# Four recurrent layers on one core: layer 0's first chain moved from GpSimd to VectorE, and layer 2's inside-chunk weights held without the quarter that causality makes zero

## The chip, the cores and the metric

One core of one Trainium2 chip. The metric is the device time of one execution in microseconds (us), on the one core that the kernel uses. Three executions of the kernel before took 1184.43, 1192.12 and 1193.15 us (median 1192.12). A change of 1% is about 12 us.

## The reference, cut to what matters

The program is four layers over X of shape 2 batches x 1024 positions x 128 features; each layer computes `x = x + s * silu(g)` with a sequence part `s` and a mixture or feed-forward part `g`. Two places matter here.

Layer 0 normalises x, adds a gated residual, quantises it in groups, normalises again (`u`) and runs a selective scan (Mamba) on it. Its step size passes through a softplus before the scan can begin:

```
xs = silu(conv(u @ in_proj.T))            # 4 taps
dt, B, C = split(xs @ x_proj.T)
dt = softplus(dt @ dt_proj.T + dt_b)
h = h * exp(dt * A) + dt * x * B          # per position: the scan
```

Layer 2 is a state-space layer with 32 heads of 64 values and a state of 128. The kernel cuts the 1024 positions into 8 chunks of 128. Inside a chunk the output is a product with a weight matrix per head, zero where the source comes after the target:

```
M[s, l] = (B_s . C_l) * exp(sum of A*dt over s < k <= l)    for s <= l, else 0
Y_diag[l] = sum over s of M[s, l] * dt_s * h_s
Y_off[l]  = (C_l . state before the chunk) * exp(sum of A*dt up to l)
y = (Y_diag + Y_off + D*h) * silu(gate), then a norm and W_out
```

M has 128 sources (s) by 128 targets (l) per chunk. For targets in the first half of a chunk, the sources of the second half are all zero: that is one quarter of M.

## The kernel before, in words

The kernel is written layer by layer, but the order in which each engine works is not the order of the text. `_operations` (line 153) collects every instruction with a cost (`_price`, line 104), `_forward` (line 259) plays the program out with these costs, the tiles' buffers and the semaphores' lags, `_backward` gives each operation how much work still hangs on it, and `_issue_order` (line 433) runs both in turn 30 times, then 300 times with random changes of the keys, and keeps the shortest order that its own costs give. That order is forced on all engines. So a change in one place can reorder the whole program. Costs for PE in `_price`: a plain f32 product takes 8 ns plus 4 x 0.4167 ns for each column of the moving operand; of products that write 64, 32 or 8 partitions, those that follow each other into the same tile (`mate`, line 213) are counted as running beside each other, and the last of them takes 87 ns more. A change between array shapes elsewhere has no cost in the plan.

Layer 0 begins with four stages per 512 positions (normalise, turn, gate, residual), then `quantise`, then the parts of the scan's input for one half of a batch (512 positions): `take_1` (line 1000: statistics, inverse root, `u`, its transpose and the split in two f32r halves `uT_h`, `uT_l`), `take_2` (taps and silu), `take_3` (projection, `dt`), `take_4` (line 1071: softplus, `dt` to DRAM) and `take_5`. `statistics` (569) calls `inverse_root` (579): three Newton steps, which for four columns (`small_pool`) run on GpSimd as 12 small instructions (lines 595 to 598), and else on VectorE as 9 (591 to 593). In `take_1` the four `u` (line 1007) are GpSimd's, in `take_4` two operations for each half of the channels (1080, 1081). The scan (`step`, 1246) cannot begin before `take_4` of the first half is through and `dd` has come back by DMA. Beside all this run the steps of layer 0's mixture of experts (`first`, `second`, `third`, `weighted_sum`, lines 1127 to 1162).

Layer 2 works in 32 blocks (2 batches x 16 blocks; a block is 128 feature rows, two heads). `batch_start` (1487) makes, once per batch, B and C, the products `GT` of B and C in each chunk (1510, 1512), and the sums of A*dt as rows that it writes to DRAM (`Vd`, `Cd`, `So`). For each block, `front` (1659) makes h and the gate, `weights` (1684) M, `states` (1704) the chunk states, and `tail` (1740) the output. In the main loop `front` and `weights` run two blocks ahead of `tail`.

`weights`: two small DMAs bring the rows of the two heads (`Srow` from `Cd`, `Mrow` from `Vd`); for each half of the chunks two products over 512 columns (line 1698) make the exponents of both heads in PSUM, ScalarE takes exp over 1024 columns (1699), VectorE multiplies with `GT` (1701) into `M`, 128 partitions x 1024. `tail`: for each half (`q`) of the positions, eight products with 64 output partitions each (line 1757, two heads side by side, 128 sources, 128 targets) into `yd`, four with all 128 partitions (1762) into `yo`; VectorE adds D*h (1765) and multiplies by the decay (1767); GpSimd adds and gates (1768, 1769); ScalarE squares. `yd`, `yo` and `wo` share two PSUM banks (tag `y_ps`). Every fourth block the gated blocks go through `W_out` (1781).

All DMAs are issued by SP, one queue in order.

Of the kernel before, what the change touches and what calls it, by code (L numbers as in the profile page):

```python
# [10 lines left out]
F32 = mybir.dt.float32  # L11
# [8 lines left out]
P = 128  # L20
# [131 lines left out]

def _operations(nc, slots):
# [6 lines left out]
    for ins in nc.cur_bb.bb.instructions:  # L160
# [7 lines left out]
        if ins.opcode == "Matmult" and not ins.is_transpose and writes[0].ap[0][1] in (8, 32, 64):  # L168
            op.strip, op.area = writes[0].offset // (writes[0].ap[0][0] or 1), 1.0
            op.columns, op.strips = {(op.strip, writes[0].offset)}, {op.strip}  # L170
# [43 lines left out]
        if op.columns and mate is not None and mate.columns and mate.tiles[-1] == op.tiles[-1] and not mate.columns & op.columns:  # L214
            op.columns |= mate.columns
            if op.strip in mate.strips:
                op.cost += 10.0
            else:
                op.strips |= mate.strips
                op.cost = 25.0  # L220
            first = mate.first
            first.after.update({o: max(lag, first.after.get(o, -1e3)) for o, lag in op.after.items() if o.at < first.at})
            mate.mate, op.first = op, first
# [235 lines left out]
def recurrent_d4(ctx: ExitStack, tc: tile.TileContext, x, w0, f0, fwd, w1, w13d, w1y, w2, w2in, w3, r0, r2, r3, out):  # L459
# [109 lines left out]
    def statistics(src, ts):  # L569

        n = len(ts)
        st = small.tile([P, n, 6], F32, name=f"ln_st{n}")
        mv = small.tile([P, n, 2], F32, name=f"ln_mv{n}")
        for i, t in enumerate(ts):
            nc.vector.bn_stats(st[:, i, :], src[:, t, :])
            nc.vector.bn_aggr(mv[:, i, :], st[:, i, :])
        return mv, inverse_root(mv[:, :, 1], f"ln{n}")

    def inverse_root(v, name):

        n = v.shape[-1]
        small_pool = n == 4
# [7 lines left out]
        for _ in range(0 if small_pool else 3):  # L590
            nc.vector.tensor_tensor(t, y, y, ALU.mult)  # L591
            nc.vector.scalar_tensor_tensor(t, t, -0.5, x, ALU.mult, ALU.mult)
            nc.vector.scalar_tensor_tensor(y, t, 1.5, y, ALU.add, ALU.mult)
        for _ in range(3 if small_pool else 0):
            nc.gpsimd.tensor_tensor(t, y, y, ALU.mult)
            nc.gpsimd.tensor_tensor(t, t, x, ALU.mult)
            nc.gpsimd.tensor_scalar(t, t, -0.5, 1.5, ALU.mult, ALU.add)
            nc.gpsimd.tensor_tensor(y, t, y, ALU.mult)
# [226 lines left out]
    with ExitStack() as l1, ExitStack() as l0:  # L825
# [52 lines left out]
        with pool_of("l0a") as pa, pool_of("l0b", bufs=2) as pb, pool_of("l0_pre", bufs=5, space=PSUM) as pp:  # L878
# [121 lines left out]
            def take_1(b, h, pp, tag):  # L1000

                ts = range(b * TPB + 4 * h, b * TPB + 4 * h + 4)
                mv, rinv = statistics(qx, ts)
                shift = shifted(mv, rinv)
                u = pj.tile([P, 4, D], F32, name="u")
                for j, t in enumerate(ts):
                    nc.gpsimd.tensor_scalar(u[:, j, :], qx[:, t, :], rinv[:, j : j + 1], shift[:, j : j + 1], ALU.mult, ALU.add)
# [63 lines left out]
            def take_4(b, h, pp, tag, fast=False):  # L1071
# [3 lines left out]
                for c in range(2):  # L1075
# [4 lines left out]
                    nc.gpsimd.tensor_scalar(w[:, c, :], e, 1.0, -1.0, ALU.add, ALU.add)  # L1080
                    nc.gpsimd.tensor_tensor(w[:, c, :], e, w[:, c, :], ALU.subtract)
# [29 lines left out]
            take_1(0, 0, pp, "mm")  # L1111
# [230 lines left out]
    with ExitStack() as l2, ExitStack() as lead:  # L1342
# [79 lines left out]
        with pool_of("w2early", side="right") as pe, pool_of("l2f", side="right") as pf, pool_of("l2fw", bufs=2, side="right") as pw, lead:  # L1422
# [42 lines left out]
            le_from = pa.tile([P, 4, P], F32, name="le_from")  # L1465
# [5 lines left out]
            for b in range(4):  # L1471
                nc.gpsimd.tensor_copy(le_32[:, 32 * b : 32 * (b + 1)], le_from[:, b, 32 * b : 32 * (b + 1)])

# [7 lines left out]
            Mrow = [pfr.tile([P, 4, P], F32R, name=f"Mrow{i}", bufs=1) for i in range(NR)]  # L1481
# [5 lines left out]
            def batch_start(b, room, pw, pp):  # L1487
# [15 lines left out]
                GT = pa.tile([P, TPB, P], F32, name=f"GT{b}")  # L1503
                for q in range(2):
                    ps = pp.tile([P, W], F32, name="bt_ps", tag="pre")[:, :512]
                    pg = pp.tile([P, W], F32, name="g_ps", tag="pre")[:, :512]
                    for j in range(4):
                        c = slice((4 * q + j) * P, (4 * q + j + 1) * P)
                        nc.tensor.transpose(ps[:, j * P : (j + 1) * P], Bf[:, c], ident)
                        nc.tensor.matmul(pg[:, j * P : (j + 1) * P], Bf[:, c], Cf[:, c], start=True, stop=True)  # L1510
                    nc.scalar.copy(Btok[:, 4 * q : 4 * q + 4, :], ps.rearrange("p (j d) -> p j d", d=P))
                    nc.vector.tensor_tensor(GT[:, 4 * q : 4 * q + 4, :], pg.rearrange("p (j d) -> p j d", d=P), le.unsqueeze(1).to_broadcast([P, 4, P]), ALU.mult)
# [7 lines left out]
                for half in range(2):  # L1520
                    ps = pp.tile([P, W], F32, name="v_ps", tag="pre")[:, :512]
                    pk = pp.tile([P, W], F32, name="k_ps", tag="pre")[:, :512]
                    for o, x, m, first, last in ((ps, Adt, le_from.rearrange("p b l -> p (b l)"), True, True), (pk[:, :P], Adt, le_32, True, False), (pk[:, :P], nlog, ident, False, True)):
# [3 lines left out]
                    pv = ps.rearrange("p (b l) -> p b l", b=4)  # L1527
                    v.append(room("v2", [P, 2, 4, P], F32R))
                    split(pv, v[half][:, 0], v[half][:, 1])
                    nc.scalar.activation(so[:, half, :], pv[:, 0, :], AF.Exp)  # L1530
                    yield
                    mark(f"start_2_{b}")
                Vd = pd.tile([4, NH, 2, 8, P], F32, name="Vd")
                Cd = pd.tile([NH, 2, 4, 2, P], F32, name="Cd")
                So = pd.tile([NH, 2, 4, P], F32, name="So")
                for half in range(2):
                    nc.sync.dma_start(Vd[:, :, half].rearrange("c h o l -> (c h) o l"), v[half].rearrange("p o b l -> p (o b) l").bitcast(F32))
                    nc.sync.dma_start(Cd[:, half].rearrange("h c o k -> c h (o k)"), csum[:, half].rearrange("p o k -> p (o k)").bitcast(F32))
# [59 lines left out]
            patm = pf.tile([8, 512], F32, name="patm", tag="rows")  # L1598
# [6 lines left out]
            pm1 = patm.rearrange("r (c l) -> r c l", c=4)  # L1605
            nc.gpsimd.memset(pm1, -1.0)
            for sign, off in ((1, 0), (-1, 1)):
                nc.gpsimd.affine_select(out=pm1, in_=pm1, pattern=[[-2 * sign, 4], [0, P]], compare_op=ALU.is_ge, fill=0.0, base=off, channel_multiplier=sign)
            for Sr, Mr in zip(Srow, Mrow):
                nc.vector.tensor_tensor(Sr[:32].rearrange("r g k -> r (g k)"), pat, pat2, ALU.add)  # L1610
                nc.vector.tensor_copy(Mr[32:40].rearrange("r c l -> r (c l)"), patm)
# [42 lines left out]
        with pool_of("l2mid") as pmid, pool_of("l2w", bufs=2) as pw, pool_of("l2end", bufs=3) as pend, pool_of("l2_in", bufs=2, space=PSUM) as pin, pool_of("l2_ps", bufs=2, space=PSUM) as pp:  # L1654
# [29 lines left out]
            def weights(b, i):  # L1684
# [7 lines left out]
                nc.sync.dma_start(Sr[32:40].bitcast(F32), Cd[hs].rearrange("h a c o k -> (c o) (h a) k"))  # L1692
                nc.sync.dma_start(Mr[:32].bitcast(F32), Vd[:, hs].rearrange("c h a o l -> (h a o) c l"))
                Ms = [pw.tile([P, 2, 512], F32, name="M", bufs=6) for _ in range(2)]
                for half, M in enumerate(Ms):
                    ps = pin.tile([P, 2, 512], F32, name="e_ps", tag="pre")
                    for h in range(2):
                        nc.tensor.matmul(ps[:, h, :], Sr[:, 2 * h + half, :], Mr.rearrange("r c l -> r (c l)"), start=True, stop=True)  # L1698
                    nc.scalar.activation(ps, ps, AF.Exp)  # L1699
                    G = GT[:, 4 * half : 4 * half + 4, :].rearrange("p j l -> p (j l)").unsqueeze(1).to_broadcast([P, 2, 512])  # L1700
# [3 lines left out]
            def states(b, i):  # L1704
# [4 lines left out]
                htok = pw.tile([P, TPB, P], F32, name="htok")  # L1709
                hdd = pmid.tile([P, TPB, P], F32, name="hdd")  # L1710
                cd = pmid.tile([P, 2, 2, HP * 4], F32, name="cd", bufs=2)
                nc.sync.dma_start(cd.rearrange("p a h w -> p a (h w)"), Dd[:, 2 * i : 2 * i + 2].rearrange("a h p j -> a (h p j)").partition_broadcast(P))
                for half in range(2):
# [8 lines left out]
                    nc.scalar.copy(htok[:, js, :], ps.rearrange("p (j f) -> p j f", j=4))  # L1722
                    nc.gpsimd.tensor_tensor(v(hdd[:, js, :]), v(htok[:, js, :]), by(dtd), ALU.mult)  # L1723
# [14 lines left out]
                mid_of[b, i] = (mid_of[b, i], htok, stc)  # L1738

            def tail(b, i):  # L1740
# [7 lines left out]
                Ms, htok, stc = mid_of.pop((b, i))  # L1748
                so = pend.tile([P, S], F32, name="so2")
                for k in range(2):  # L1750
                    nc.sync.dma_start(so[64 * k : 64 * (k + 1)], So[2 * i + k].rearrange("a c l -> (a c l)").partition_broadcast(64))
                for q in range(2):
                    cols = slice(512 * q, 512 * (q + 1))
                    yd = pp.tile([P, 512], F32, name="yd_ps", tag="y_ps")
                    for j in range(4):
                        for k in range(2):
                            nc.tensor.matmul(yd[64 * k : 64 * (k + 1), j * P : (j + 1) * P], htok[:, 4 * q + j, 64 * k : 64 * (k + 1)], Ms[q][:, k, j * P : (j + 1) * P], start=True, stop=True)  # L1757
                    yo = pp.tile([P, 512], F32, name="yo_ps", tag="y_ps")
                    for j in range(4):
                        c = 4 * q + j  # L1760
                        if c:
                            nc.tensor.matmul(yo[:, j * P : (j + 1) * P], stc[:, c - 1, :], Cf[:, c * P : (c + 1) * P], start=True, stop=True)  # L1762

                    y = h[:, cols]
                    nc.vector.scalar_tensor_tensor(y, y, W2["D"][:, i : i + 1], yd, ALU.mult, ALU.add)  # L1765
                    a = P if q == 0 else 0
                    nc.vector.tensor_tensor(so[:, 512 * q + a : 512 * (q + 1)], yo[:, a:], so[:, 512 * q + a : 512 * (q + 1)], ALU.mult)  # L1767
                    nc.gpsimd.tensor_tensor(y[:, a:], y[:, a:], so[:, 512 * q + a : 512 * (q + 1)], ALU.add)  # L1768
# [3 lines left out]
                    else:  # L1772
                        nc.scalar.activation(so[:, cols], y, AF.Square)  # L1773
                        nc.gpsimd.tensor_tensor(ssq[:, cols], ssq[:, cols], so[:, cols], ALU.add)  # L1774
# [41 lines left out]
            places = dict(Bf=("M", 6), v2=("M", 6), rows=("so2", 3), cdx=("cd", 2))  # L1816
# [231 lines left out]
```

## Time and profile before

| what | us |
|---|---|
| median of three executions | 1192.12 |
| the profiled execution: its own time | 1188.86 |
| its span, first to last instruction | 1187.1 |
| layer 0 (to about 460), of it before the first exp of the scan (line 1251) | 118.1 |
| layers 1 and the start of 2 | about 460 to 670 |
| layer 2's blocks | about 670 to 1095 |
| layer 3, whose first work lies beside the last blocks | to 1187 |

The page gives, per engine, the busy time and its share of the span, and by 40 slices how busy each engine was and the granted clock of TensorE (1.0 is full speed). PE is TensorE's matrix work, PEld its weight loads, which may run beside it; DVE is VectorE, ACT ScalarE, POOL GpSimd, SP the engine that issues DMAs. A f32 product appears as two records (x16 is eight products), an f32r product as one. The records' durations contain the way through the array, so how densely products follow each other is read from their starts. Over the whole span PE is busy 1020.7 us (86%), DVE 931.5 (78%), ACT 866.1 (73%), POOL 739.2 (62%). The granted clock is below full speed in some stretches between 100 and 450 us and between 600 and 692 us; from 700 us on it is 1.0.

### The profile page before, as it was taken

The page shows a single profiled execution, that of the slowest core. Times are in us where ns is not written, and L with a number is a line of the kernel's source. Part 1 is how long each engine was busy: PE and PEld are TensorE (multiplying, and loading weights), DVE is VectorE, ACT ScalarE, POOL GpSimd, SP SyncE. Part 2 cuts the span into 40 slices and gives each one's busy share as a digit, 9 for nine tenths or more (in the row PEclk, how much of TensorE's full clock was granted, in tenths as well). Part 3 has the DMA queues.
Part 4 walks back from the last instruction along what each step waited for, and adds up shares of the span by engine and source line. Part 5 has one row for each costly group of instructions (what it writes and reads, how often), then busy time and mean ns, then how long its engine had stood idle before and what let it go on. Part 6 is the DMA issues. An engine that isn't in the chain of part 4 may idle for free.

```text
span 1187.1 us, 18167 instructions
## 1 busy us (share of the span) xinstructions
PE 1020.7 (86%) x6399; PEld 735.6 (62%) x6399; DVE 931.5 (78%) x1537; ACT 866.1 (73%) x1294; POOL 739.2 (62%) x776
## 2 busy tenths in 40 slices
PE   3997967979376889989779789999998999998998
PEld 2664523435033666778658576867676777776787
DVE  6734798997899896675776488888888999888666
ACT  4556785785877894574847689888898988877654
POOL 6564598895987375232151158797995978899311
PEclk9998997999567989999959899999999999999999
DMA  3003445352552113020030333445354444442000
GB/s 109 8 21 101 125 120 182 123 186 99 189 177 83 51 62 100 1 82 23 5 106 32 87 100 96 111 119 149 101 141 95 125 107 112 107 111 73 19 9 28
DMA packets 58846, 109.09 MB, mean 92 GB/s; under 512 B 6274, under 2 KB 31746, under 8 KB 58628
## 3 DMA queue, kind: packets, MB, share of 16 engines
q1 hardware_dynamic: 58756, 107.93, 31.6%
q8 instruction: 51, 0.84, 0.3%
q14 instruction: 39, 0.32, 0.1%
HBM read 91.52 MB, written 14.29 MB: 89 GB/s over the span
## 4 chain that ended last, share of the span: by engine, by line
PE 34%; DVE 10%; ACT 9%; issue 4%; DMA 3%; POOL 2%; SPq 0%; POOLq 0%; DVEq 0%; ACTq 0%
PE wo_ps L1781 4%; PE yd_ps L1757 3%; PE u_ps L1734 3%; PE yo_ps L1762 3%; DVE h L1419 2%; PE e_ps L1698 2%; PE y_ps L799 2%; DVE st L1735 2%; PE ht_ps L1719 1%; DMA so<-So 1%; PE y_ps L1895 1%; PE y_ps L1646 1%; PE av_ps L1925 1%; ACT e_ps L1699 1%; DVE M L1701 1%
## 5 line engine op out<-in xcount | busy, mean ns | idle before, releaser
L1256 POOL TENSOR_TENSOR hs<-hs,bc 128x512 f32<-128x512 f32 x128 | 161.0, 1278 | 48.6 <-DVE hs L1252 28.8
L1419 DVE SCALAR_TENSOR_TENSOR h<-in_ps,w,h 128x1023 f32<-128x1023 f32 (+2 forms) x96 | 121.1, 1271 | 5.7 <-ACT h L1416 5.5
L1251 ACT ACTIVATE dA<-dd,negA 128x512 f32<-128x512 f32 x128 | 87.4, 688 | 31.8 <-DVE hs L1252 25.4
L1735 DVE TENSOR_TENSOR_SCAN st<-cd,u_ps 128x512 f32<-128x512 f32 x64 | 77.8, 1215 | 19.4 <-PE u_ps L1734 8.7
L1701 DVE SCALAR_TENSOR_TENSOR M<-e_ps,GT 128x1024 f32<-128x1024 f32 x64 | 77.0, 1214 | 10.5 <-ACT e_ps L1699 10.3
L1768 POOL TENSOR_TENSOR h<-h,so 128x384 f32<-128x384 f32 (+1 forms) x64 | 73.0, 1144 | 19.1 <-DVE so L1767 18.6
L1769 POOL TENSOR_TENSOR h<-h,sg 128x512 f32<-128x512 f32 x64 | 82.9, 1300 | 0.8
L1252 DVE TENSOR_TENSOR_SCAN hs<-dA,last,dBx 128x512 f32<-128x512 f32 x64 | 79.9, 1271 | 2.9 <-ACT dA L1251 2.0
L799 PEld LDWEIGHTS y_ps<-w2e,hh 128*128 128x128 f32 x512 | 72.4, 199 | 14.7 <-DVE hh L791 3.8
L799 PE MATMUL y_ps<-w2e,hh 128*128 128x128 f32 x512 | 78.1, 288 | 1.9 <-DVE acc L804 0.9
L1723 POOL TENSOR_TENSOR hdd<-htok,dtd 128x512 f32<-128x512 f32 x64 | 67.1, 1051 | 20.3 <-ACT htok L1722 15.4
L1774 POOL TENSOR_TENSOR ssq<-ssq,so 128x512 f32<-128x512 f32 x60 | 76.6, 1286 | 3.0 <-ACT so L1773 2.9
L1757 PE MATMUL yd_ps<-M,htok 128*64 128x128 f32 x1024 | 70.7, 280 | 8.0 <-DVE M L1701 5.6
L1252 DVE TENSOR_TENSOR_SCAN hs<-dA,dBx 128x512 f32<-128x512 f32 x64 | 75.7, 1211 | 2.1 <-ACT dA L1251 1.1
L1734 PEld LDWEIGHTS u_ps<-hdd,Btok 128*128 128x128 f32 x448 | 63.3, 193 | 16.8 <-issue 6.0
L1762 PE MATMUL yo_ps<-Cf,stc 128*128 128x128 f32 x448 | 70.7, 280 | 2.1 <-DVE h L1765 0.9
L1734 PE MATMUL u_ps<-hdd,Btok 128*128 128x128 f32 x448 | 69.8, 281 | 2.8 <-POOL stc L1737 1.3
L1762 PEld LDWEIGHTS yo_ps<-Cf,stc 128*128 128x128 f32 x448 | 62.3, 191 | 13.4 <-issue 4.7
L1757 PEld LDWEIGHTS yd_ps<-M,htok 128*64 128x64 f32 x1024 | 55.1, 137 | 24.4 <-issue 7.0
L1243 DVE TENSOR_TENSOR dBx<-dd,B_ps 128x1024 f32<-128x1024 f32 x48 | 57.9, 1209 | 12.2 <-PE xz_ps L623 4.7
L1699 ACT ACTIVATE e_ps<-e_ps 128x1024 f32<-128x1024 f32 x64 | 64.3, 1011 | 1.9 <-PE e_ps L1698 1.4
L1263 PE MATMUL y_ps<-hs,fold 128*32 128x512 f32 x256 | 52.9, 758 | 14.1 <-DVE ln_t L591 9.2
(535 smaller groups left out, 3190.7 us busy)
## 6 DMA issues: line engine op xcount, KB each, us to landing
bc<-BCd SPq DMA_DIRECT2D x32, 512.0 KB
cd<-Dd SPq DMA_DIRECT2D x32, 512.0 KB
so<-So SPq DMA_DIRECT2D x64, 256.0 KB
dd<-Dtd SPq DMA_DIRECT2D x28, 512.0 KB
w13f<-in_w13d_dram SPq DMA_DIRECT2D x16, 256.0 KB
Dtd<-dt SPq DMA_DIRECT2D x7, 512.0 KB
fw<-in_fwd_dram SPq DMA_DIRECT2D x16, 192.0 KB
dd<-dt SPq DMA_DIRECT2D x4, 512.0 KB
```

Source lines behind the costliest of these rows:

```text
L799: nc.tensor.matmul(y_ps[:, j * P : (j + 1) * P], hh[:, c, j * P : (j + 1) * P], w2e[:, c * P : (c + 1) * P], start=(c == 0), stop=(c == 1))
L1251: nc.scalar.activation(dA, dd[:, r, 0, :], AF.Exp, scale=negA[:, n, r : r + 1])
L1252: nc.vector.tensor_tensor_scan(hs[:, r, :], dA, dBx[:, r, :], last[:, n, r : r + 1] if h else 0.0, ALU.mult, ALU.add)
L1256: nc.gpsimd.tensor_tensor(hs[:, r, :], hs[:, r, :], cs[:, 0, :], ALU.mult)
L1419: nc.vector.scalar_tensor_tensor(dst[:, n:], ps[:, : S - n], w[:, k : k + 1], dst[:, n:], ALU.mult, ALU.add)
L1701: nc.vector.scalar_tensor_tensor(M, ps, 3.0e38, G, ALU.min, ALU.mult)
L1734: nc.tensor.matmul(pv[:, j, :], Btok[:, c, :], hdd[:, c, :], start=True, stop=True)
L1735: nc.vector.tensor_tensor_scan(st.rearrange("p f j -> p (f j)"), cd[:, half].rearrange("p h w -> p (h w)"), ps, 0.0, ALU.mult, ALU.add)
L1757: nc.tensor.matmul(yd[64 * k : 64 * (k + 1), j * P : (j + 1) * P], htok[:, 4 * q + j, 64 * k : 64 * (k + 1)], Ms[q][:, k, j * P : (j + 1) ...
L1762: nc.tensor.matmul(yo[:, j * P : (j + 1) * P], stc[:, c - 1, :], Cf[:, c * P : (c + 1) * P], start=True, stop=True)
L1769: nc.gpsimd.tensor_tensor(y, y, sg[:, cols], ALU.mult)
L1774: nc.gpsimd.tensor_tensor(ssq[:, cols], ssq[:, cols], so[:, cols], ALU.add)
```

## The change

1. Layer 0: `statistics` and `take_1` get a flag `fast`, as `take_4` already had one for its first DMA; it is on for the first half of the first batch alone. With it the inverse root (9 instead of 12 small instructions), the four `u` and the softplus' two operations per half of the channels run on VectorE instead of GpSimd.
2. Layer 2: `M` is 128 x 2 x 384 instead of 128 x 2 x 512. For four chunks it holds four second halves of targets (64 columns each, all 128 sources) and two blocks of 64 columns in which the first halves of two chunks share the partitions: the even chunk's 64 sources in the lower half, the odd chunk's in the upper half. `GT`, the row tables and the patterns are made to fit (`pack`, `mask`, `patm`, `patm2`); `Vd` and `Cd` get two rows more, written by 32 further DMAs in all (8 more for each half of a batch).
3. `states` copies the first 64 sources of the odd chunks to the upper partitions by two DMAs per block (`hodd`), 64 in all.
4. `tail`: 16 products of 64 output partitions per block become 32: sixteen of all 128 sources by 64 targets, and sixteen of 64 sources by 64 targets, which use a quarter of the array each. Even chunks go to one bank, odd ones to the other, so VectorE's operations take every second chunk, and GpSimd's follow after both.
5. The planner: the products that write 64 partitions or less are told apart by quarter (`cells`) and may be mates across two tiles of the same kind.
6. Buffers: `Bf` of the second batch takes an `h2` buffer instead of an `M` buffer; `le_from` lies in a shorter-lived pool.

```
+    def statistics(src, ts, fast=False):
-        return mv, inverse_root(mv[:, :, 1], f"ln{n}")
+        return mv, inverse_root(mv[:, :, 1], f"ln{n}", n == 4 and not fast)
...
-                    nc.gpsimd.tensor_scalar(u[:, j, :], qx[:, t, :], rinv[:, j : j + 1], shift[:, j : j + 1], ALU.mult, ALU.add)
+                    (nc.vector if fast else nc.gpsimd).tensor_scalar(u[:, j, :], ...)
...
-                    nc.gpsimd.tensor_scalar(w[:, c, :], e, 1.0, -1.0, ALU.add, ALU.add)
-                    nc.gpsimd.tensor_tensor(w[:, c, :], e, w[:, c, :], ALU.subtract)
+                    eng = nc.vector if fast else nc.gpsimd
+                    eng.tensor_scalar(w[:, c, :], e, 1.0, -1.0, ALU.add, ALU.add)
+                    eng.tensor_tensor(w[:, c, :], e, w[:, c, :], ALU.subtract)
...
-            take_1(0, 0, pp, "mm")
+            take_1(0, 0, pp, "mm", True)
...
-                Ms = [pw.tile([P, 2, 512], F32, name="M", bufs=6) for _ in range(2)]
+                Ms = [pw.tile([P, 2, 384], F32, name="M", bufs=6) for _ in range(2)]
...
-                        nc.tensor.matmul(ps[:, h, :], Sr[:, 2 * h + half, :], Mr.rearrange("r c l -> r (c l)"), start=True, stop=True)
+                        nc.tensor.matmul(ps[:, h, :384], Sr[:, 2 * h + half, :], Mr, start=True, stop=True)
+                    ps = ps[:, :, :384]
...
+                    nc.sync.dma_start(hodd[up, 2 * half : 2 * half + 2, :], htok[lo, 4 * half + 1 : 4 * half + 4 : 2, :])
...
+                yds = [pp.tile([P, 512], F32, name="yd_ps", tag="y_ps") for _ in range(2)]
+                for j in range(4):
+                    M, at = Ms[j // 2], 256 + 64 * (j % 2)
+                    for k in range(2):
+                        c = 2 * j + k
+                        for a, f in enumerate(heads):
+                            nc.tensor.matmul(yds[k][f, j * P + 64 : (j + 1) * P], htok[:, c, f], M[:, a, 64 * (c % 4) : 64 * (c % 4) + 64], start=True, stop=True)
+                    for yd, x, rows in ((yds[0], htok[lo, 2 * j], lo), (yds[1], hodd[up, j], up)):
+                        for a, f in enumerate(heads):
+                            nc.tensor.matmul(yd[f, j * P : j * P + 64], x[:, f], M[rows, a, at : at + 64], start=True, stop=True)
+                for k, yd in enumerate(yds):
+                    nc.vector.scalar_tensor_tensor(hk[:, k], hk[:, k], W2["D"][:, i : i + 1], yd.rearrange("p (c l) -> p c l", l=P), ALU.mult, ALU.add)
+                for k in range(2):
+                    yo = pp.tile([P, 512], F32, name="yo_ps", tag="y_ps")
+                    for j in range(1 - k, 4):
+                        c = 2 * j + k
+                        nc.tensor.matmul(yo[:, j * P : (j + 1) * P], stc[:, c - 1, :], Cf[:, c * P : (c + 1) * P], start=True, stop=True)
+                    nc.vector.tensor_tensor(sk[:, k, 1 - k :], yo.rearrange("p (c l) -> p c l", l=P)[:, 1 - k :], sk[:, k, 1 - k :], ALU.mult)
-                    yd = pp.tile([P, 512], F32, name="yd_ps", tag="y_ps")
-                    for j in range(4):
-                        for k in range(2):
-                            nc.tensor.matmul(yd[64 * k : 64 * (k + 1), j * P : (j + 1) * P], htok[:, 4 * q + j, 64 * k : 64 * (k + 1)], Ms[q][:, k, j * P : (j + 1) * P], start=True, stop=True)
...
```

The order of the changed kernel's instructions is known before it runs, since the planner fixes it. In the tails it is not the order of the text: the planner may take a product whose mate is not ready later, and mostly does the even chunks' tile first, alternating between the two new forms of product, then the odd chunks'.

## The prediction

> **What bounds the kernel now.** I read the page's groups, then the busy time by stretch. In layer 2's main stretch the granted clock is 1.00 and TensorE is the fullest engine:
>
> ```profile
> core 0: us, PE busy (x) PEld busy (x) DVE busy (x) ACT busy (x) POOL busy (x), PEclk, DMA share, GB/s
> 700.00:1090.00 390.00, 371.05 (x2737) 284.88 (x2738) 346.06 (x397) 337.89 (x438) 323.06 (x315) 1.00 0.44 114
> ```
>
> PE is idle for 19 of 390 us, VectorE for 44, ScalarE for 52, GpSimd for 67. What shortens VectorE or ScalarE lies under PE; what lengthens PE has 19 us of room, and little more. The groups that the change touches there:
>
> ```profile
> L1701 DVE SCALAR_TENSOR_TENSOR M<-e_ps,GT 128x1024 f32<-128x1024 f32 x64 | 77.0, 1214 | 10.5 <-ACT e_ps L1699 10.3
> L1757 PE MATMUL yd_ps<-M,htok 128*64 128x128 f32 x1024 | 70.7, 280 | 8.0 <-DVE M L1701 5.6
> L1699 ACT ACTIVATE e_ps<-e_ps 128x1024 f32<-128x1024 f32 x64 | 64.3, 1011 | 1.9 <-PE e_ps L1698 1.4
> ```
>
> Then PE's timeline, for what it costs to change the shape in which the array is used. In layer 0's mixture two shapes alternate (128 rows x 8 columns, 8 x 128):
>
> ```profile
> 282.61 0.27 PE L1186 MATMUL se_ps<-ident,sel 128*8 128x128 f32 x1
> 282.82 0.48 PE L1191 MATMUL go_ps<-vT,selT 8*128 8x128 f32 x2
> 283.23 0.27 PE L1186 MATMUL se_ps<-ident,sel 128*8 128x128 f32 x1
> ```
>
> The reader is to look at the starts. From 282.61 to 283.23 are 0.62 us for three records of 128 columns, which within one shape come every 0.11 us (layer 0's eight L1154 records at 71.99 are followed by the next product at 72.90). So 0.62 - 0.33 = 0.29 us go into two changes: **0.145 us each**. A change of the rows alone costs it too:
>
> ```profile
> 197.57 0.47 PE L623 MATMUL p<-xh,fw_h 128*128 128x512 f32 x1
> 197.97 0.49 PE L1152 MATMUL p<-b,ones_r 64*128 64x512 f32 x1
> 198.39 0.82 PE L1154 MATMUL p<-fw,h 128*128 128x128 f32 x5
> ```
>
> L623 with 512 columns takes 0.23 us in a stream (850.00 to 850.23), here 0.40 until the 64-row product begins, and that one 0.42 until the 128-row product begins: 0.17 and 0.19 us more.
>
> Layer 0's start, GpSimd's and VectorE's timelines:
>
> ```profile
> 72.65 1.75 POOL L1007 TENSOR_SCALAR u<-qx,ln_y,shift 128x128 f32<-128x128 f32 x4
> 99.75 3.84 POOL L1080 TENSOR_SCALAR sp_w<-sp_e 128x512 f32<-128x512 f32 x2
> 103.55 2.49 POOL L1081 TENSOR_TENSOR sp_w<-sp_e,sp_w 128x512 f32<-128x512 f32 x2
> 104.85 0.70 DVE L1082 TENSOR_TENSOR ln_ps<-ln_ps,sp_w 128x512 f32<-128x512 f32 x1 [4.26 <-POOL sp_w L1081]
> ```
>
> Until the scan's first exp at 118.1 us all is one chain; GpSimd sits in it twice.
>
> **Layer 0.** (a) The Newton steps begin on GpSimd at 55.06 us and, among other work, `u` is done at 74.40; on VectorE nine small instructions of 0.17 to 0.30 us and four `u` of 0.34 (row L643 on VectorE) are some 4 us, so `u` could be there near 61. What follows is then PE's order. Before, the taps (`xz_ps`) begin at 82.14, right after the transposes of the second routing (81.99), which come 7.8 us after that routing's first product (74.20). In the changed order this routing stands behind the eighth second-layer product of the mixture, not the eleventh; its like ended before 67.12 (66.06 + 1.06). 67 + 7.8 = 74.8, against 82.1: -7.3 us. (b) The softplus: on VectorE two operations of 0.41 (L1105, 512 columns) and two of 0.69 are 2.2 us, hidden by ScalarE's table load and Ln (98.80 to 101.39); the wait of 4.26 us goes. Late next is Ln itself. Sum -11.6 us. Given back: two to three steps of the mixture (2.7 us of PE each: 73.78 to 79.20 are two) move into the scan, where PE is free (26 to 44 of 50 us) but ScalarE is busy 33 to 41 of 50. VectorE's 6 us more fall into a stretch where it is busy 25 of 50 us. I take **-10**, from -4 (only the 4.26) to -13.
>
> **Layer 2, TensorE.** In the order of the changed kernel's instructions the 1024 products of the tails stand in 463 runs of one form (236 of 128 sources, 227 of 64), nearly all of two products: 337 changes between the forms, 126 into them from others, 126 out. Before: 64 runs, 64 in, 64 out. That is 337 + 62 + 62 = 461 changes more. No row shows this very pair, 128x64 against 64x64; the rows above change columns and rows, or rows alone, and cost 0.145 to 0.19. The lower end is 0, the upper 0.19; I take 0.15, since 64-column weights lie between the 8 and 128 of the first row: 461 x 0.15 = **+69 us** (0 to +88).
>
> Streaming: before, 256 pairs side by side, two records each of 0.109 (16 records in 1.09 us): 256 x 0.218 = 55.8. After: 256 pairs and 227 steps of quarters (198 pairs, 29 fours) of 64 columns. A record of one column comes every 0.03 us (L1543, 16 from 845.63 to 846.13), of 128 every 0.109; half of the latter is 0.055, which I take for 64: 483 x 0.109 = 52.6, **-3.2** (-27 at 0.03 each, +49 at 0.109).
>
> Row 128 x L1698: 512 to 384 columns, a quarter of 0.23: -0.058 x 128 = **-7.4**. Sum for PE +58 us.
>
> A floor per product could undo even the streaming. The 16 records of L1162 at 80.59 take 0.62 us, so 0.039 a record, below half of yd's step for two. [...]
>
> **Layer 2, the rest.** M: 1214 ns for 1024 columns, 681 for 512 (L658): 1.04 ns a column, 256 fewer, x64 = -17 us on VectorE. Exp: 1011 against 601 (L1022, 512 columns): 0.80 ns, -13 us on ScalarE. Both are hidden by PE: 0 (to -5, if waits of DVE at 10.5 shrink). GpSimd's adds now wait for both halves of a block; two blocks stand between: 0 (to +5). `hodd`: 64 DMAs more on SP, 0.3 us each as `Mrow`'s (302 to 318 ns), 19 us of an SP that idles; behind it stand `cd`, `so` and the row tables, and it waits itself for ScalarE's copy. `states` runs two blocks, some 26 us, ahead of `tail`: 0 (to +10, 0.3 us for each of 32 blocks, if PE meets it late). The 32 DMAs in `batch_start` are 10 us of SP; the first batch's rows leave at 615.6 and are read at 671.9, which covers it; the second lies beside blocks: 0 (to +3). `pack`, `mask` and patterns are GpSimd's at 580 to 630, busy 13 of 50: 0.
>
> How much of +58 shows: PE's 19 us idle are waits for others, and VectorE's and ScalarE's relief shortens some; I let half of it (10 us) take up work: **+48**. At the least all 19 and as much again hidden in the records' own length (0.27 us against steps of 0.11): +20. At the most +58 and the +10 of hodd.
>
> **Sum** against the profiled execution, 1188.9: -10 + 48 = **1227 us**. It stands 3 us under the median of 1192.1; the later runs should spread likewise.
>
> **The rivals.** *The two forms do not hinder each other* (0.14): the array would keep its two columns of 64, and only the row half in use changes. Then 337 x 0.15 = 51 us vanish, PE is +7, which its idle time covers, and layer 2 gains some 5 from shorter exp and M: 1188.9 - 10 - 5 = 1174, faster. It decides from a price of about 0.04 us between the forms: 7.4 + 337 x 0.037 = 20, what idle time (10) and layer 0 (10) give. Against it stands L1152, where only the rows change. [...] *They do, but PE's slack takes most* (0.13): +20, 1199, no difference. *The plan goes wrong besides* (0.13): the planner has no cost for these changes, so what it placed to meet is late; with hodd's 10 and 10 for later tails 1247. *That the first half's move does nothing*: layer 0 would give 0 if PE's order, not `u`, held the taps; it is inside the range.
>
> **How the numbers follow.** The main case has 0.60 and gives 1227 (its own range 1212 to 1243). A measurement here tells 1% (12 us) from no change. Faster is the first rival, 0.14. Same is the second, 0.13. Slower is the rest, 0.73. The range 1190 to 1252 leaves out the first rival and about 0.05 above.
>
> **What would show it.** Changes between the forms: starts in PE's timeline of 0.25 us for a run of one pair, not 0.11. PE in the main stretch near 95% still, VectorE's idle time grown, the stretch of blocks some 48 us longer. M near 950 ns, exp near 800. Scan's first exp near 107. Wrong would be: runs of pairs every 0.11 us; PE waiting for DMA `hodd`; or VectorE the fullest engine.

## The result: 6.2% slower, and the profile after

The changed kernel takes 1260.34 us (median of four executions, 1258.03 to 1268.86), beside it the kernel before 1188.68 us (four, 1184.43 to 1193.15): a ratio of 1.062, 95% interval 1.058 to 1.067. The forecast was 1227 with 1252 as its upper end. The profiled execution took 1261.7 us, with a span of 1260.0.

Where the time lies is read from the first and last starts of a few tiles in the two timelines (us from the span's start):

| | before | after | difference |
|---|---|---|---|
| first exp of the scan (`dA`) | 118.1 | 106.8 | -11.3 |
| last scan of layer 0 (`hs`, VectorE) | 447.8 | 451.4 | +3.6 |
| last accumulation of layer 1's mixture (`acc`, VectorE) | 587.9 | 595.5 | +7.6 |
| first product of a tail (`yd`) | 677.2 | 689.5 | +12.3 |
| last product of a tail | 1091.6 | 1162.8 | +71.2 |
| end | 1187.1 | 1260.0 | +72.9 |

So 12.3 us are lost before the blocks, 58.9 in them, 1.7 behind them. First the main stretch, in the window that the prediction showed (the kernel after, busy time by stretch):

```profile
core 0: us, PE busy (x) PEld busy (x) DVE busy (x) ACT busy (x) POOL busy (x), PEclk, DMA share, GB/s
700.00:1090.00 390.00, 380.77 (x3156) 285.28 (x3155) 290.94 (x346) 294.44 (x386) 267.96 (x262) 0.97 0.45 107
```

PE is idle for 9 us of 390 instead of 19; VectorE, which was idle for 44, now is for 99. PE alone sets the pace. The groups say what it does (the kernel after, groups of instructions; last come the idle time before them and what ended it):

```profile
L1797 PE MATMUL yd_ps<-M,htok 128*64 128x64 f32 x1024 | 82.2, 251 | 1.4 <-DVE so L1809 1.4
L1734 DVE SCALAR_TENSOR_TENSOR M<-e_ps,GT 128x768 f32<-128x768 f32 x64 | 59.7, 949 | 13.7 <-ACT e_ps L1732 13.5
L1732 ACT ACTIVATE e_ps<-e_ps 128x768 f32<-128x768 f32 x64 | 50.3, 795 | 7.0 <-PE e_ps L1730 6.4
L1803 DVE SCALAR_TENSOR_TENSOR h<-h,w,yd_ps 128x512 f32<-128x512 f32 x64 | 47.3, 743 | 43.5 <-PE yd_ps L1800 43.2
L1800 PE MATMUL yd_ps<-M,hodd 64*64 64x64 f32 x512 | 44.0, 250 | 0.0
L1800 PE MATMUL yd_ps<-M,htok 64*64 64x64 f32 x512 | 43.8, 249 | 0.0
```

The tails' products were 70.7 us of PE and are 82.2, 44.0 and 43.8 in three groups; these overlap, and together they cover 135.8 us. M and exp became as short as was worked out (949 and 795 ns), and it is worth nothing: VectorE waits 43 us for those products (L1803). In the kernel before, the same operation waited 4.6 us for them (its groups of instructions):

```profile
L1765 DVE SCALAR_TENSOR_TENSOR h<-h,w,yd_ps 128x512 f32<-128x512 f32 x64 | 47.2, 738 | 5.6 <-PE yd_ps L1757 4.6 <-POOL h L1768 0.9
```

PE's timeline of one tail (the kernel after; start, duration of the group, x16 is eight products):

```profile
start us, us, engine line op out<-in xcount [idle before <-releaser]
927.31 0.34 PE L1797 MATMUL yd_ps<-M,htok 128*64 128x64 f32 x4
927.58 0.33 PE L1800 MATMUL yd_ps<-M,hodd 64*64 64x64 f32 x4
927.84 0.34 PE L1797 MATMUL yd_ps<-M,htok 128*64 128x64 f32 x4
928.11 0.33 PE L1800 MATMUL yd_ps<-M,hodd 64*64 64x64 f32 x4
928.37 0.50 PE L627 MATMUL g_ps<-xh,w_in_l 128*128 128x512 f32 x1
```

One pair of products takes 0.26 us from start to start. An f32 product is two records, here called two passes; inside a form passes come 58 ns apart (seen in e4 below), so two of them, with the pair's products side by side, are 0.12 us, and 0.15 us are left for each change of form. Where this time lies shows in the single starts: the first start behind a change comes 152 ns (median of 191 changes from 128 to 64 sources) or 148 ns (146 changes back) after the last start ahead of it, where a next pass of the same form comes after 52; the second pass behind the change then comes after 100 ns instead of 52. That is 100 + 48 = 148 ns.

And the start of layer 0 (the kernel after, timelines of VectorE and ScalarE):

```profile
67.78 1.10 DVE L1013 TENSOR_SCALAR u<-qx,ln_y,shift 128x128 f32<-128x128 f32 x4
...
106.85 0.69 ACT L1258 ACTIVATE dA<-dd,negA 128x512 f32<-128x512 f32 x1 [3.44 <-DMA dd<-dt]
```

`u` begins 4.9 us sooner (72.65 before), the scan's first exp comes 11.3 us sooner. At layer 0's last scan, 345 us later, nothing of it is left.

### The profile page after: what moved, and what is told of

It is laid out like the page before. It is cut to its first block, busy times and chain, and to the rows that moved or that the text cites. A ratio compares the mean times of both kernels' runs of the same rounds, so it can differ in the third digit from the quotient of the medians.

```text
span 1260.0 us, 20476 instructions
## 1 busy us (share of the span) xinstructions
PE 1092.9 (87%) x7455; PEld 793.8 (63%) x7455; DVE 938.2 (74%) x1558; ACT 855.5 (68%) x1294; POOL 728.7 (58%) x763
## 4 chain that ended last, share of the span: by engine, by line
PE 59%; DVE 13%; ACT 13%; POOL 6%; issue 4%; DMA 4%; SPq 0%; POOLq 0%; DVEq 0%; ACTq 0%
PE yd_ps L1797 5%; PE yd_ps L1800 5%; PE wo_ps L1826 4%; PE u_ps L1769 4%; PE y_ps L805 3%; PE yo_ps L1808 3%; PE ht_ps L1753 2%; PE e_ps L1730 2%; ACT L1258 2%; POOL hs L1263 2%; ACT L796 2%; DVE hs L1259 2%; ACT dA L1258 2%; PE p L1161 1%; PE g_ps L627 1%
## 5 line engine op out<-in xcount | busy, mean ns | idle before, releaser
L1426 DVE SCALAR_TENSOR_TENSOR h<-in_ps,w,h 128x1023 f32<-128x1023 f32 (+2 forms) x96 | 121.5, 1272 | 12.3 <-ACT h L1423 11.9
L1797 PE MATMUL yd_ps<-M,htok 128*64 128x64 f32 x1024 | 82.2, 251 | 1.4 <-DVE so L1809 1.4
L1803 DVE SCALAR_TENSOR_TENSOR h<-h,w,yd_ps 128x512 f32<-128x512 f32 x64 | 47.3, 743 | 43.5 <-PE yd_ps L1800 43.2
L1769 PE MATMUL u_ps<-hdd,Btok 128*128 128x128 f32 x448 | 74.0, 292 | 1.4 <-POOL hdd L1758 0.9
L1797 PEld LDWEIGHTS yd_ps<-M,htok 128*64 128x64 f32 x1024 | 50.2, 141 | 34.1 <-issue 14.3
L1734 DVE SCALAR_TENSOR_TENSOR M<-e_ps,GT 128x768 f32<-128x768 f32 x64 | 59.7, 949 | 13.7 <-ACT e_ps L1732 13.5
L1808 PE MATMUL yo_ps<-Cf,stc 128*128 128x128 f32 x448 | 67.5, 282 | 0.0
L796 ACT ACTIVATE hh<-pg 128x512 f32<-128x512 f32 x64 | 37.7, 597 | 42.0 <-PE pg L629 39.2
```

Source lines behind the costliest of these rows:

```text
L1426: nc.vector.scalar_tensor_tensor(dst[:, n:], ps[:, : S - n], w[:, k : k + 1], dst[:, n:], ALU.mult, ALU.add)
L1769: nc.tensor.matmul(pv[:, j, :], Btok[:, c, :], hdd[:, c, :], start=True, stop=True)
L1797: nc.tensor.matmul(yds[k][f, j * P + 64 : (j + 1) * P], htok[:, c, f], M[:, a, 64 * (c % 4) : 64 * (c % 4) + 64], start=True, stop=True)
```

## The experiments

Theory: each change of the array's shape costs PE 0.15 us on the path, and the 12 us before the blocks belong to the redrawn order, not to layer 0's part itself. Rivals: small products cost a fixed time whatever their form; the two tiles filled at once or `hodd`'s transfers hold the tails; layer 0's part itself costs time. Each run's ratio is against the kernel before on the same chip. "Changes" are counted in PE's records of each trace: between the two forms, and into and out of the tails' products (the counts in the expectations are up to four lower). Stretches and starts are those of the one profiled execution, which can lie some us off the median.

**e1, layer 0's part alone** (the kernel before with item 1 of the change).

> The kernel before with layer 0's part of the change alone. The changed kernel's first exp of the scan came 11.3 us earlier, but its last scan ended 3.6 us later than before. Theory A (the chain is shorter, and the lead is spent in the order of the work beside the scan and in layer 1): first exp near 107 us, the whole within 8 us of before's 1188.7. Theory B (the -10 of the prediction is real and is hidden in the changed kernel by something of layer 2): first exp near 107, whole 1177 to 1181.

1194.4 us, ratio 1.004 (1.001 to 1.008). First exp at 105.1 us, last scan 442.9 (-4.9), last `acc` 575.0 (-12.9), first tail product 674.2 (-3.0), end +4.4. The lead of 13 us is there, and all but 3 us of it is gone by the blocks. Theory A, as worded.

**e2, layer 2's part alone.**

```
-            take_1(0, 0, pp, "mm", True)
+            take_1(0, 0, pp, "mm")
...
-                    eng = nc.vector if fast else nc.gpsimd
+                    eng = nc.gpsimd
```

> The changed kernel with layer 0's part undone. If layer 2's part carries the loss by itself (blocks +59 us in the trace): 1245 to 1268, first exp of the scan back at 118 us. If the two parts together upset the order of the first 680 us (first e_ps came 8.6 us later than before): 1240 to 1248.

1252.5 us, 1.054 (1.050 to 1.059). The blocks begin at 677.3 us, as before (677.2), and take 464.9 us: +50.5. PE's busy time in them is 451.7 us, before 392.7: **+59.0**. So layer 2's part is the loss, and the changed kernel, with layer 0's part (-10 in the forecast), takes 8 us more by the medians. The profiled execution of e2 is the fastest of its four, 5.6 us under the median.

**e3, one form.**

```
-                    for yd, x, rows in ((yds[0], htok[lo, 2 * j], lo), (yds[1], hodd[up, j], up)):
+                    for yd, x, rows in ((yds[0], htok[:, 2 * j], slice(0, P)), (yds[1], hodd[:, j], slice(0, P))):
...
-                    nc.sync.dma_start(hodd[up, 2 * half : 2 * half + 2, :], htok[lo, 4 * half + 1 : 4 * half + 4 : 2, :])
+                    nc.sync.dma_start(hodd[:, 2 * half : 2 * half + 2, :], htok[:, 4 * half + 1 : 4 * half + 4 : 2, :])
```

> The changed kernel, but its products for the first halves of targets take all 128 rows of the array (128 sources where they should take 64, so this leaves the output wrong in these targets by terms of the neighbouring chunk; hodd is copied in full, 128 KB instead of 64). Every tail product then has one form, 128 sources by 64 targets; their number, order and columns stay nearly the same (318 steps from one kind to the other, which now change nothing). Theory (a change of form costs 0.15 us on a PE that sets the pace): 337 x 0.15 = 50 us less than the changed kernel, 1205 to 1220. Rival (small products cost a fixed time each whatever the form, or hodd's transfers hold the tails): 1250 to 1262.

1220.6 us, 1.028 (1.022 to 1.034): 40 us less than the changed kernel by the medians, at the upper edge of what the theory gave. The blocks take 437.2 us, 36 less, and PE is busy 412.2 us in them, 49 less. As many products, as many columns, a transfer twice as large, and the time goes: it is the form, not the number of small products. The 252 changes into and out of the tails' products (before 128) stay.

**e4, bank by bank.** The loop over the two banks is put outside; in each the products of 128 sources come first, then those of 64:

```
+                for k, yd in enumerate(yds):
+                    for j in range(4):
+                        c, M = 2 * j + k, Ms[j // 2]
...
+                    for j in range(4):
+                        M, at = Ms[j // 2], 256 + 64 * (j % 2)
+                        x, rows = (hodd[up, j], up) if k else (htok[lo, 2 * j], lo)
...
```

> The changed kernel with the same products written bank by bank: eight of 128 sources, then eight of 64, for the even chunks, then the same for the odd ones. In the order of its instructions 75 changes between the two forms are left of 337, and 106 changes into and out of the tails' products of 236. Theory (0.15 us a change): 392 fewer are 59 us less, 1200 to 1215; what of it does not show is PE's idle time coming back. Rival (changes between the forms cost nothing where one bank is used, the price lies in 1024 more records): 1250 to 1262.

1185.1 us, 0.998 (0.995 to 1.001): 75 us less than the changed kernel, by the order of some lines. The blocks take 408.6 us, 65 less; another 13 us lie ahead of them, in the order that was redrawn (first tail product at 676.5 us, not 689.5). One bank in PE's timeline (the kernel by banks):

```profile
904.52 0.52 PE L1796 MATMUL yd_ps<-M,htok 128*64 128x64 f32 x12
904.97 0.68 PE L1801 MATMUL yd_ps<-M,htok 64*64 64x64 f32 x16
905.58 0.50 PE L629 MATMUL g_ps<-xh,w_in_h 128*128 128x512 f32 x1
```

Eight products of 64 sources take 0.61 us with one change, where in the changed kernel two take 0.26. The whole is more than the 59 us expected: 13 us come from ahead of the blocks, and in the blocks the granted clock loses 14 us less (last section).

**e12, alternating.** The same as e4, but inside a bank a pair of each form in turn.

> The kernel written by banks, but inside a bank the two forms alternate chunk by chunk. The same products, tiles, operations and transfers; in the order of its instructions 461 changes between the forms where writing by banks has 75, and 102 into and out of them (106). Theory (0.15 us a change on the path): 382 x 0.15 = 57 us more than by banks (1185), less what PE's idle time takes up: 1225 to 1242, the blocks' stretch 448 to 466 us. Rival (what cost the changed kernel its time was the two tiles filled at once, not the changes): 1180 to 1200.

1252.5 us, 1.053 (1.048 to 1.059): 67 us more than by banks, the blocks 478.4 us (+69.8), outside what was expected (1225 to 1242), to the costly side. First the main stretch of the kernel by banks:

```profile
690.00:1085.00 395.00, 378.57 (x3735) 299.80 (x3732) 331.07 (x398) 326.61 (x439) 321.76 (x313) 1.00 0.47 122
```

Then that of the alternating kernel:

```profile
690.00:1140.00 450.00, 437.23 (x3685) 336.71 (x3686) 336.92 (x397) 332.94 (x441) 317.75 (x310) 0.96 0.42 104
```

PE is full again, and the granted clock is 0.96 instead of 1.00. Added up over the blocks that is some 20 us of lost clock (last section); 70 less 20 is 50, or 0.13 us for each of 378 changes more (0.18 if all of it is theirs). One bank at a time, no transfer altered: the rival of the two tiles falls.

**e9 and e10, fours.** Both banks' products of 128 sources first, then all of 64, four side by side; the planner keeps the order:

```
             mate.mate, op.first = op, first
+            if _kind(op) == "yd_ps" or "yd_ps" in op.tiles[-1]:
+                op.after.setdefault(mate, -1e3)
```

> Both parts in, and the tails' products always in one order: eight of 128 sources for the even chunks, eight for the odd ones, then all sixteen of 64 sources, four side by side (the planner is made to keep this order). In the order of its instructions there are 32 changes between the forms, and 92 into and out of them: 124, where writing by banks had 181. The changed kernel's trace shows two steps of four in 275 ns where two steps of a pair take 262 ns, so four stream in the time of two: 128 fours instead of 256 pairs are 128 x 0.109 = 14 us less. Theory (changes and streaming set the pace of PE): 57 x 0.15 + 14 = 22 us less on PE than by banks (1185), of which half to all shows: 1163 to 1175. Rival (the two banks are then held together, and VectorE's four operations per block come late and bunched): 1180 to 1200, with VectorE's idle time before its operations on the banks grown.

> The same without layer 0's part. So far the pairs with and without it differ by +7, +8, +10 and -21 us. If the draw of the plan decides: any difference within 20 us of e9, the scan's first exp at 118 us. If layer 0's part costs 7 us by itself: 7 shorter than the kernel with it.

e9: 1191.4 us, 1.002 (0.999 to 1.005); e10, without layer 0's part: 1216.9, 1.023 (1.019 to 1.026). PE got part of the relief. The main stretch of e9:

```profile
700.00:1090.00 390.00, 356.80 (x3597) 274.85 (x3596) 324.63 (x386) 315.71 (x422) 311.83 (x302) 1.00 0.50 119
```

The longest waits of the other engines in its blocks (e9; us in total, times, longest):

```profile
POOL h L1816 <- DVE so L1812: 29.7, 15, 7.1
DVE M L1736 <- ACT e_ps L1734: 19.9, 11, 3.9
ACT htok L1758 <- PE ht_ps L1755: 18.0, 15, 3.7
```

PE is busy 357 us of 390, by banks 373, but a little less work lies in this window (3597 records, by banks 3644). Over the whole stretch of the blocks PE is busy 382.6 us, by banks 390.9: the relief is 8 to 17 us, of the 22 worked out for streaming and changes. The blocks became no shorter (420.0 us, by banks 408.6); PE's idle time in them grew from 18 to 37 us. PE is no longer what sets the pace; no engine is full, and the time lies in waits between them. The theory's 1163 to 1175 is missed. The rival holds in its sum, though VectorE's wait for the banks (7.1 us, by banks 8.4) did not grow as it said.

**e5 to e8, other draws.** e5 is e4 without layer 0's part; e6, e7, e8 are the kernel before, e1 and e4 with `random.Random(2)` in place of 1.

> The kernel written bank by bank, without layer 0's part. With layer 0's part undone the changed kernel was 8 us shorter, and layer 0's part alone made the kernel before 7 us longer. Theory A (layer 0's part costs some 7 us wherever it stands): 1185 - 7 = 1178. Theory B (those 7 and 8 us are the draw of the plan and of the granted clock, not the part): anywhere from 1178 to 1195, with the first exp of the scan back at 118 us and the blocks' stretch (first to last product of the tails) still 404 to 414 us.

> The kernel before, its plan drawn with another start of the random numbers: the same instructions in another order. It measures what the draw alone moves. Theory B (the draw is worth as much as layer 0's part): 3 to 10 us off 1187.6 in either direction. Theory A (the draw is worth little): 1185 to 1190.

> The kernel before with layer 0's part alone, with the same other start of the random numbers. To be read against that kernel before with the same start. Theory A (layer 0's part costs 7 us): 5 to 9 us longer than it. Theory B (the draw decides): any other difference, as likely shorter; the scan's first exp near 107 us in either case.

> The kernel written bank by bank, layer 0's part in, with the other start of the random numbers. If the gain of writing by banks (75 us against the changed kernel) is that of the array's shapes and not of a lucky draw, it stays within 1178 to 1198 and the blocks' stretch within 404 to 418 us.

| | us | ratio (95%) | first exp | last scan | first tail product | blocks' stretch |
|---|---|---|---|---|---|---|
| e5 | 1206.6 | 1.014 (1.010 to 1.018) | 119.7 | 457.7 | 689.0 | 415.7 |
| e6 | 1187.2 | 0.999 (0.996 to 1.002) | 119.2 | 446.7 | 672.2 | 415.5 |
| e7 | 1197.4 | 1.006 (1.001 to 1.011) | 109.2 | 449.4 | 680.5 | 418.0 |
| e8 | 1185.9 | 0.997 (0.995 to 1.000) | 108.5 | 444.0 | 668.1 | 420.7 |

Another start of the random numbers changes little (-2 to +3 us), so "the draw" was the wrong word. But any change of the program redraws the order of everything, and that moves the time by up to some 25 us: with layer 0's part against without it, the five pairs differ by +7, +10 (seed 2), +8 (in the changed kernel), -21 (by banks) and -26 us (fours). The three small ones stand little above the spread of the runs (each ratio's interval is 0.3 to 0.5% to either side, 4 to 6 us); the two large ones are clear of it. e5 came out above what either theory gave, e10 differs from e9 by more than the 20 us expected, and the blocks of e5 and e8 are 2 and 3 us over their ranges.

**e11, e13, e14: the part with the order held.** The planner takes the moved instructions for GpSimd's, draws the order of the kernel without them, and they join VectorE at their planned starts. PE's records then stand in the same order to the last of 6399 (e13 against e2, e14 against e5: 7455).

```
+        if ins.name in _MOVED:
+            self.engine = "Pool"
...
+    orders["Pool"] = [op for op in orders["Pool"] if op not in moved]
+    orders["DVE"] = sorted(orders["DVE"] + moved, key=lambda op: best[2][op])
```

> Layer 0's part alone, with the order of the kernel before held: the planner is told that the moved instructions are still GpSimd's (the inverse root keeps its 12 small instructions), so it draws the very plan of before, and VectorE's order takes them in at their planned starts. PE, ScalarE and SP have the order of before, instruction by instruction. Theory A (the loss of 7 to 10 us that this part brought was the redrawn order): no longer than before, 1180 to 1189, first exp of the scan at 110 to 115 us, last scan at 442 to 448 us. Theory B (the part itself costs it, by VectorE's 6 us more): 1192 to 1198.

> The changed kernel, both parts in, but with the order that is drawn for it without layer 0's part (1252.5 us) held: the moved instructions join VectorE's order at their planned starts. Theory A (the 8 us between these two are the redrawn order): 1243 to 1252, the first product of the tails at 671 to 677 us as without the part (677.3), not at 689.5. Theory B (the part loses time in the changed kernel): 1257 to 1263.

> The kernel written by banks with layer 0's part, but with the order that is drawn without it (1206.6 us) held. With its own order it takes 1185. Theory A (the order makes the 21 us, the part 2 to 6): 1199 to 1206. Theory B (the part is worth the 21 us here): 1182 to 1190.

e11 (in the order of before): 1185.3 us, 0.996 (0.992 to 0.999). First exp 116.1 us (-2.0, less than expected), last scan -3.1, first tail product -2.5, end -3.7: what the part gains it keeps. e13 (the changed kernel in e2's order): 1254.7, 1.055 (1.051 to 1.060), against e2's 1252.5; its first tail product comes at 681.3 us, e2's at 677.3, the changed kernel's at 689.5. e14 (e4 in e5's order): 1207.7, 1.017 (1.014 to 1.019), against e5's 1206.6. With the order held the part is worth -5 to +2 us, with 4 to 8 us of uncertainty each; the larger differences come with the redrawn orders. (The pairs of fours and of the other start were not run with the order held.) e14's median lies 2 us above what theory A gave and far from B; e13's lies 3 us above A and 2 under B and does not decide by itself, and its first tail product comes 4 us later than A gave. Of the 12 us that the changed kernel loses before the blocks, 8 come with the redrawn order (689.5 against 681.3 us); which of its placements costs them was not found. Part of it shows in the clock: the granted clock, averaged over all executions, is 0.930 in the changed kernel and 0.944 and 0.943 in e2 and e13, which share one order; by banks it is 0.945 (e4), and 0.936 and 0.932 in e5 and e14, which share another. Whether the clock costs the time or follows from the waits that an order brings is not shown. e11 has the lowest ratio of all, 0.4% under the kernel before; those of e4 and e8 lie within its interval.

## Why the prediction missed

Its sum was -10 + 48 = +38; it became +12.3 + 58.9 + 1.7 = +72.9.

- **Layer 0, the failed step.** "Given back: two to three steps of the mixture" and VectorE's 6 us were the whole allowance, "-4 (only the 4.26) to -13" the range. Wrong was that a lead at 107 us is still one at 680: I read the new order only up to the first exp, although the planner redraws it to the end. At the first tail product the -10 had become +12.3; the five pairs above put the part, with its redrawn order, between -26 and +10, and with the order held it is -5 to +2. That is 22 of the 35 us by which the sum fell short, and the range left out that this term could be positive.
- **The -11.6 up to the first exp** came as -11.3, in part by luck. `u` began at 67.8 us, not near 61, since VectorE had other work between the Newton steps, and the taps at 77.2 instead of 82.1: -4.9, not -7.3. Behind the taps it was -6.4, not -4.3. In the same paragraph "PE is free (26 to 44 of 50 us)" misreads the windows: those are PE's busy times, so 6 to 24 us of 50 were free.
- **The price of a change, 0.15 us:** right (148 ns in the trace at full clock; 0.13 to 0.18 from e12). The number of changes was 445 more than before in the changed kernel's trace, 462 in e2's, for the 461 of the sum. The rival that the forms do not hinder each other is refuted by e3, e4 and e12.
- **PE +58 and +48 shown:** right, where the clock stays near 1.00: e2 has +59.0 of PE's busy time and +50.5 of time, with 3 us of clock lost in the blocks. The changed kernel has +68.9 and +58.9, with 16 us of clock lost where the kernel before loses 2. The sum held the clock at 1.00; the surplus of some 10 us goes with it.
- **The rival "the plan goes wrong besides"** (1247) came nearest in number, but it priced late tails and `hodd`, not an order redrawn ahead of the blocks.
- **M, exp, `hodd`, the adds on GpSimd:** 0, as taken. M and exp hit their durations, and PE waits for `hodd` nowhere in the changed kernel.
- **A quarter of M saved:** the streaming term (-3.2) was small, and by the 58 ns a pass of e4 it is about 0, because a product of 64 sources costs PE as many passes of 58 ns as one of 128 unless four run together. Where they always do (e9), it is, with fewer changes, 8 to 17 us of PE, and then PE is not the bound. No version had the whole program shorter by it.

The number of changes orders the kernels, once the clock lost in the blocks (last section) is taken off:

| kernel | changes | PE busy in the blocks' stretch | the stretch | clock lost in it | the stretch less that |
|---|---|---|---|---|---|
| fours (e9) | 126 | 382.6 | 420.0 | 2 | 418 |
| before | 128 | 392.7 | 414.4 | 2 | 413 |
| by banks (e4) | 185 | 390.9 | 408.6 | 2 | 407 |
| one form (e3) | 252 | 412.2 | 437.2 | 5 | 432 |
| alternating (e12) | 563 | 464.6 | 478.4 | 22 | 456 |
| changed | 573 | 461.6 | 473.3 | 16 | 458 |
| layer 2's part alone (e2) | 590 | 451.7 | 464.9 | 3 | 462 |

Below some 185 changes the stretch does not follow them. From 185 to 590 it grows by 55 us, 0.135 us for each change.

## What to carry to other kernels

Count the changes of the array's shape in the order that really runs, price them from the starts in a timeline, and group products of one form before cutting their size: here the same products cost 65 to 70 us more or less in the blocks by the order of a loop. Where a planner orders the whole program, a local gain is a claim on the local stretch alone: hold the old order to measure the edit, and give any redrawn order a range of both signs (here up to some 25 us).

## What was not expected of the hardware

PE's granted clock fell to one half inside the blocks, where in the kernel before it was 1.00 from 680.9 us on. The kernel after, busy time by stretch:

```profile
945.00:950.00 5.00, 3.75 (x24) 2.86 (x23) 4.96 (x8) 4.08 (x6) 1.87 (x4) 1.00 0.53 96
950.00:955.00 5.00, 3.38 (x15) 2.07 (x15) 4.76 (x9) 4.96 (x6) 1.14 (x2) 0.81 0.85 222
955.00:960.00 5.00, 4.73 (x53) 3.28 (x53) 2.54 (x4) 3.03 (x4) 2.37 (x1) 0.50 0.60 136
960.00:965.00 5.00, 5.00 (x37) 4.30 (x34) 3.65 (x10) 2.67 (x4) 0.00 (x0) 0.67 0.29 85
965.00:970.00 5.00, 5.00 (x59) 3.83 (x57) 3.15 (x6) 4.95 (x7) 3.15 (x3) 1.00 1.00 220
```

The reader is to look at PE's busy time ahead of the fall, which comes at 953.1 us: 3.75 and 3.38 of 5 us, with no idle stretch above 0.83 us. In this trace the granted clock is 1.00 or 0.50, and stays so for whole steps of 3.41 us (here three at 0.50, from 953.1 to 963.3 us). In the step ahead of this fall PE was idle for 1.4 us, in pieces. Another fall of the same trace, at 1086.2 us, has no idle time in the step ahead of it at all:

```profile
1080.00:1085.00 5.00, 5.00 (x60) 3.98 (x58) 4.54 (x7) 4.94 (x7) 3.11 (x4) 1.00 0.40 111
1085.00:1090.00 5.00, 5.00 (x44) 4.47 (x41) 1.43 (x2) 1.91 (x3) 3.83 (x4) 0.66 0.07 15
```

In that step PE's records touch, but 12 changes lie between them. In the blocks of the four kernels with over 500 changes (the changed one, e2, e12, e13) 8 of 14 falls are like this, with 12 or 13 changes and at most 0.02 us of idle time in the step ahead. In the blocks of the twelve other kernels all 20 falls follow a step with 1.3 to 2.6 us of idle time and at most 2 changes. What brings the clock down is not shown: in the blocks of the changed kernel three steps at full clock hold 12 changes and no idle time, and a fall follows two of them; in those of the kernel before four steps hold 1.4 to 1.7 us of idle time, and none follows; e2, with the most changes, has two falls. No run tested it.

Added up (time by one less the clock), the blocks of the changed kernel lose 16 us to it, those of e12 22, of e2 3, of before and e4 under 2. At half clock a change costs more as well: in the changed kernel, from 956.8 to 960.8 us, passes inside a form come 107 ns apart instead of 58, and a change adds 198 ns instead of 148 (the next start comes after 243 ns instead of 100, the second pass after 162 instead of 107); in e5, at 1091 us, these are 107 and 199.

Products that use different parts of the array start 5 to 8 ns apart (the tails of the changed kernel), and four of 64 by 64 (0.625 us for the sixteen products of a tail in e9) take hardly longer than two (0.612 us for eight in e4).
